# Two graph layers in one kernel: order of the passage between batches, PSUM pairs by turns, and another bank for batch 0's second heads

## The chip, the cores and the metric

The kernel runs on one core of one Trainium2 chip, as one program. The metric is the device time of one execution in microseconds. Before the change it is 3888.36 us (median of 3 runs, 3888.07 to 3892.78).

## What is computed

The input x has 8 batches of 2048 nodes with 256 features; adj is one 2048 x 2048 matrix of zeros and ones, used for all batches. All arithmetic is in f32. Cut to what matters:

```python
# layer 0: 4 heads of 64, softmax within each chunk of 256 keys, summed over 8 chunks
q, k, v = x @ Wq.T + bq, x @ Wk.T + bk, x @ Wv.T + bv
s = clip(q . k / 8, -10, 10);  s = where(adj == 0, -10, s)
ctx = sum over chunks of softmax(s in the chunk) @ v
y = layernorm(ctx @ Wo.T + bo + x) * gamma + beta
x1 = layernorm(x + y)
# layer 1: 4 heads of 64, additive attention over all neighbours
Wh = x1 @ W;  e = leaky_relu(s_src[i] + s_dst[j], 0.2);  e = where(adj, e, -inf)
out = layernorm(x1 + elu(softmax_j(e) @ Wh))
```

## The kernel before

Layer 0 of batch b and layer 1 of batch b-1 run side by side. The loop over b (L854) has 64 **slots** (L870): 4 groups of 512 query nodes, 2 pairs of heads, 8 chunks of 256 keys; 16 slots make one query group. Every engine executes its instructions in the order in which this Python code emits them (a manual schedule, L88); the tile pools and semaphores decide only how long each waits. So the order of the code is the order of the work on each engine.

One slot s does this. `scores(s + 1)` (L350): for each of two 128-key tiles u, two matmuls (one for each head) into a PSUM pair `ps` (2 banks), then on DVE the clip and mask into `pr` (L371). `product(s, 0)` and `product(s, 1)` (L385): the matmuls of one head into `pc`, one bank of pool psC, which has one buffer, and the copy to `raw` on ACT (L400). Between them on ACT stand `exps(s + 1, u)` (L381), two exponentials. `normalize(s - 1)` (L402) stands ahead of the scores: a reciprocal `rd` on DVE, then a product and a sum on POOL.

Between the two products there is the side work of the slot. In batch 0 that is a piece of the mask preparation (`Masks.step`, L201, as long as there are pieces): transposes into `pm` in pool psL, a clip on DVE and a cast `edge` on ACT. From batch 1 on it is `Layer1.step` (L754): three tiles, each with one DVE instruction that makes the edge weights `e` (L689) from `srow`, a row read back from device memory (`rowD`), and 10 or 12 matmuls into `pa` (pool psL, L709). The tiles used in a slot are made in the slot before; three are made ahead of slot 0 (L864). When a unit of layer 1 is finished, `close` (L726) is done in four steps, one for each call of `rest`.

`Between` (L482) takes a finished query group from context to layer 1 input: bias, output projection `po`, add, two norms (statistics on DVE, the power on POOL, the application on ACT), and `values`, the product x1 @ W in `pw`. For groups 0 to 2 its steps are spread over the slots of the next group (tables L570 to L589). `Closing` and `Close` (L760 to L794) do the last norm of layer 1 of two batches before, in the first slots from batch 2 on.

For the last group, and for the projections of the next batch, there is a **passage** between two batches (L923 to L969): the list `order`, written out by hand, 7 times in all. A projection of node group g (`project`, L289) has five pieces: l loads x by 8 DMAs on SP, t turns it on DVE into `xT` (L274), k, v and q are the three products (16 or 8 matmuls each; `linear` L300, `values` L316), each into one PSUM pair of pool psA, which ACT empties. I write k0, v0, q0 for group 0, and so on. `turn_all` (L541) transposes y on PE into a pair (`pt`, L283) and copies it to `x1T`. `factors` gives three small steps for the weights of layer 1.

[...] psA two pairs (one tag, two buffers: the pool chooses which), psC one bank, psL two, psM one. `ps`, `pp`, `pv`, `po` and `pw` of two or four tiles, and `pt` of y share psA.

## Time and profile before

| what | us |
|---|---|
| median of 3 runs | 3888.36 |
| the profiled execution: its time | 3890.5 |
| the profiled execution: its span | 3888.7 |
| batch 0, first scores to last slot | 73 to 414 |
| passages, start of the last `pw` of the slots | 413.8, 871.4, 1334.0, 1794.9, 2256.2, 2717.1, 3178.0 |
| PE busy | 3696.5 (95%) |
| DVE busy | 3204.7 (82%) |
| ACT busy | 1946.2 (50%) |
| POOL busy | 1384.4 (36%) |
| mean granted TensorE clock | 0.992 |

A row of the timeline gives start, length, engine, line, operation, output and inputs, and in brackets the idle time of that engine just before and what ended it. PEld is the loading of weights, which runs beside the matmuls. A matmul in f32 shows as two instructions. Ends of matmuls are modelled, so distances from start to start are the safer measure.

### The profile page before, as it was taken

The page shows a single profiled execution, that of the slowest core. Times are in us where ns is not written, and L with a number is a line of the kernel's source. Part 1 is how long each engine was busy: PE and PEld are TensorE (multiplying, and loading weights), DVE is VectorE, ACT ScalarE, POOL GpSimd, SP SyncE. Part 2 cuts the span into 40 slices and gives each one's busy share as a digit, 9 for nine tenths or more (in the row PEclk, how much of TensorE's full clock was granted, in tenths as well). Part 3 has the DMA queues.
Part 4 walks back from the last instruction along what each step waited for, and adds up shares of the span by engine and source line. Part 5 has one row for each costly group of instructions (what it writes and reads, how often), then busy time and mean ns, then how long its engine had stood idle before and what let it go on. Part 6 is the DMA issues. An engine that isn't in the chain of part 4 may idle for free. (4 is left out here: it accounts for less than half of the span.)

```text
span 3888.7 us, 160154 instructions
## 1 busy us (share of the span) xinstructions
PE 3696.5 (95%) x72068; PEld 2752.5 (71%) x72068; DVE 3204.7 (82%) x4810; ACT 1946.2 (50%) x3601; POOL 1384.4 (36%) x1202
## 2 busy tenths in 40 slices
PE   7988999999999999999999999999999999999787
PEld 4655577776777767776777767777677776776676
DVE  4776499985999779996999959998599977998798
ACT  3655445554555445554555545555455555555321
POOL 0444234342433333432433324434243333434310
PEclk9999999999999999999999999999999999999999
DMA  7642333333434343333433334333343334333354
GB/s 151 150 108 59 77 96 98 97 89 94 121 97 102 75 121 101 99 102 70 134 99 100 97 87 129 101 95 88 94 121 102 98 78 118 106 95 88 95 146 123
DMA packets 771328, 398.48 MB, mean 102 GB/s; under 512 B 442576, under 2 KB 735824, under 8 KB 770640
## 3 DMA queue, kind: packets, MB, share of 16 engines
q1 hardware_dynamic: 720640, 354.54, 35.9%
q10 hardware_dynamic: 50000, 33.70, 2.7%
q8 instruction: 563, 9.22, 1.0%
q14 instruction: 125, 1.02, 0.1%
HBM read 331.22 MB, written 56.89 MB: 100 GB/s over the span
## 5 line engine op out<-in xcount | busy, mean ns | idle before, releaser
L371 DVE SCALAR_TENSOR_TENSOR pr<-ps,slab 128x1024 f32<-128x1024 f32 x1024 | 1192.7, 1205 | 237.3 <-PE ps L360 234.0
L393 PEld LDWEIGHTS pc<-vaug,pr 128*64 128x64 f32 x32768 | 1041.6, 138 | 475.3 <-ACT raw L400 243.9
L689 DVE SCALAR_TENSOR_TENSOR e<-srow,gd,et 128x640 f32<-128x640 f32 (+1 forms) x1536 | 1348.0, 934 | 5.4 <-PE pa L709 5.4
L393 PE MATMUL pc<-vaug,pr 128*64 128x65 f32 x32768 | 1161.4, 224 | 68.9 <-ACT raw L400 63.1
L383 ACT ACTIVATE pr<-pr 128x1024 f32<-128x1024 f32 x1024 | 1052.1, 1057 | 249.3 <-DVE pr L371 234.5
L709 PE MATMUL pa<-waug,e 128*64 128x65 f32 x32768 | 1089.8, 224 | 41.0 <-DVE e L689 39.2
L709 PEld LDWEIGHTS pa<-waug,e 128*64 128x64 f32 x32768 | 1025.2, 139 | 70.3 <-DVE e L689 39.8
L360 PE MATMUL ps<-qT,kT 64*128 64x512 f32 x4096 | 1022.4, 617 | 9.1 <-DVE pr L371 7.0
L415 POOL TENSOR_TENSOR part<-raw,rd 128x512 f32<-128x512 f32 x448 | 467.9, 1044 | 1472.7 <-DVE rd L408 1460.1
L400 ACT COPY raw<-pc 128x260 f32<-128x260 f32 x1024 | 383.5, 375 | 1139.0 <-PE pc L393 1092.4
L417 POOL TENSOR_TENSOR acc<-acc,part 128x512 f32<-128x512 f32 x448 | 574.0, 1281 | 35.2
L360 PEld LDWEIGHTS ps<-qT,kT 64*128 64x128 f32 x4096 | 351.5, 186 | 332.1 <-issue 208.7
L408 DVE RECIPROCAL rd<-raw 128x8 f32<-128x8 f32 x512 | 101.5, 198 | 139.4 <-ACT raw L400 133.2
L415 POOL TENSOR_TENSOR acc<-raw,rd 128x512 f32<-128x512 f32 x64 | 66.8, 1043 | 366.1 <-DVE rd L408 365.3
L304 PE MATMUL pp<-xT,wk_sb 128*128 128x512 f32 x256 | 123.9, 628 | 47.0 <-DVE xT L274 32.3
L737 ACT ACTIVATE hh<-pa,dn 128x64 f32<-128x64 f32 x512 | 114.0, 319 | 101.3 <-DVE dn L733 101.3
L552 PE MATMUL pw<-w_sb,x1T 128*128 128x264 f32 x512 | 137.0, 403 | 2.6 <-DVE x1T L274 2.5
L468 POOL TENSOR_TENSOR rs_c<-rs_c,nhalf 128x4 f32<-128x4 f32 x32 | 55.6, 1738 | 227.5 <-DVE off_c L467 227.5
L508 PE MATMUL po<-wo_sb,qT 128*128 128x256 f32 x512 | 124.8, 389 | 0.0
L304 PEld LDWEIGHTS pp<-xT,wk_sb 128*128 128x128 f32 x256 | 48.3, 198 | 106.5 <-issue 49.6
L320 PE MATMUL pv<-wv_sb,xT 128*128 128x256 f32 x512 | 115.9, 379 | 0.0
L304 PE MATMUL pp<-xT,wq_sb 128*128 128x512 f32 x256 | 115.3, 593 | 0.0
(90 smaller groups left out, 1888.2 us busy)
## 6 DMA issues: line engine op xcount, KB each, us to landing
et<-edgeD SPq DMA_DIRECT2D x256, 320.0 KB, 3.2
slab<-clipD SPq DMA_DIRECT2D x512, 128.0 KB, 3.5
et<-edgeD SPq DMA_DIRECT2D x128, 384.0 KB, 3.5
srow<-rowD SPq DMA_DIRECT2D x64, 320.0 KB, 4.4
xp<-in_x_dram SPq DMA_DIRECT2D x256, 64.0 KB, 2.3
xg<-in_x_dram SPq DMA_DIRECT2D x32, 512.0 KB, 4.7
x1D<-y ACTq DMA_DIRECT2D x32, 512.0 KB, 3.1
x1g<-x1D SPq DMA_DIRECT2D x32, 512.0 KB, 5.9
```

Source lines behind the costliest of these rows:

```text
L304: nc.tensor.matmul(pp[:, c, :], lhsT=w[:, kc, c * P : (c + 1) * P], rhs=st["xT"][:, kc, :], start=(kc == 0), stop=(kc == KC - 1),)
L360: nc.tensor.matmul(ps[:, k, :], lhsT=kT[rows, hp, t * P : (t + 1) * P], rhs=qT[rows, hp, cols], start=True, stop=True,)
L371: nc.vector.scalar_tensor_tensor(pr, pss[u], -CLIP, slab[:, u, :].unsqueeze(1).to_broadcast([P, 2, CH]), op0=ALU.max, op1=ALU.min,)
L383: nc.scalar.activation(pr, pr, AF.Exp, scale=0.125)
L393: nc.tensor.matmul(pc[z * D : (z + 1) * D, i, :], lhsT=probs[s][u][:, k, i * P + z * D : i * P + (z + 1) * D], rhs=vaug[:, KT * c + u, 2 * ...
L400: nc.scalar.copy(raws[s][:, k], pc)
L415: nc.gpsimd.tensor_mul(part, raw[:, :, :, :D], rd.to_broadcast([P, 2, QT, D]))
L417: nc.gpsimd.tensor_add(accv, accv, part)
L508: nc.tensor.matmul(po[:, k, :], lhsT=qT[:, c, t * P : (t + 1) * P], rhs=wo_sb[:, c, :], start=(c == 0), stop=(c == KC - 1),)
L552: nc.tensor.matmul(pw[:, k, : F + 2 * H], lhsT=self.x1T[:, c, u * P : (u + 1) * P], rhs=w1_sb[:, c, :], start=(c == 0), stop=(c == KC - 1),)
L689: nc.vector.scalar_tensor_tensor(e[:, :w], self.rows[n][:, :w], self.gd[:, h, j : j + 1], self.edge[k // JG][:, j % JG, :w], op0=ALU.max, ...
L709: nc.tensor.matmul(self.pa[z * D : (z + 1) * D, i * D1 : (i + 1) * D1], lhsT=e[:, i * P + z * D : i * P + (z + 1) * D], rhs=self.waug[:, j ...
```

## The change

- psA gets two tags with one buffer each, and `two_banks` hands them out strictly by turns.
- For batches after the first, the queries of the last node group (q3) go, half by half, into the two banks of psL.
- In batch 0 `product(s, 1)` uses a bank of psL instead of psC.
- The load of group 0 of the next batch is called in slot 61 instead of 63, and its turn (t0) in slot 63 instead of in the passage.
- The first scores of a batch stand in the passage ahead of q3, their exponentials behind q3 (batch 0 keeps them where they were).
- In the passage, k1 stands ahead of q0, k2 ahead of `turn_all`; the four `lower.rest` steps are spread over the beginning of the passage.

The diff, cut to its core (`...` marks what is left out; the other uses of `two_banks` are the same edit in `transposed`, `values`, `scores`, `output` and `Between.values`):

```diff
-    psA = ctx.enter_context(tc.tile_pool(name="psA", bufs=2, space=bass.MemoryType.PSUM))
+    psA = ctx.enter_context(tc.tile_pool(name="psA", bufs=1, space=bass.MemoryType.PSUM))
...
+    turn_of = [0]
+
+    def two_banks(shape, name):
+
+        turn_of[0] ^= 1
+        return psA.tile(shape, F32, tag=f"psA{turn_of[0]}", name=name)
...
-        def linear(dst, w, bias):
-            pp = psA.tile([P, KC, CH], F32, tag="psA", name="pp")
+        def linear(dst, w, bias, apart=False):
+            if apart:
+                pps = [psL.tile([P, CH], F32, tag="psL", name="pp") for _ in range(KC)]
+            else:
+                pp = two_banks([P, KC, CH], "pp")
+                pps = [pp[:, c, :] for c in range(KC)]
...
-            lambda: linear(qT, wq_sb, bq_sb),
+            lambda: linear(qT, wq_sb, bq_sb, b > 0 and g == NCH - 1),
...
-    def product(s, k):
+    def product(s, k, alone):
...
-        pc = psC.tile([P, QT, D1], F32, tag="psC", name="pc")
+
+        pool, tag = (psL, "psL") if alone and k else (psC, "psC")
+        pc = pool.tile([P, QT, D1], F32, tag=tag, name="pc")
...
-        scores(0)
-        for u in range(KT):
-            exps(0, u)
+            scores(0)
+            for u in range(KT):
+                exps(0, u)
...
-            if s == SLOTS - 1 and b + 1 < B:
+            if s == SLOTS - 3 and b + 1 < B:
                 turns = [project(b + 1, g) for g in range(NCH)]
                 turns[0].pop(0)()
...
+            if s == SLOTS - 1 and b + 1 < B:
+                turns[0].pop(0)()
...
-            product(s, 0)
+            product(s, 0, not lower)
...
-            product(s, 1)
+            product(s, 1, not lower)
...
-        if lower and b + 1 < B:
-            lower.rest(4)
...
-            (t0, k0, v0, q0), (l1, t1, k1, v1, q1), (l2, t2, k2, v2, q2), (l3, t3, k3, v3, q3) = turns
-            order = [begin, t0, lambda: before.values((2, 3)), steps[0], k0, ctx, l1, v0, steps[1]]
-            order += [t1, steps[2], q0, *steps[3:5], k1, l2, steps[5], v1, steps[6], t2, q1, l3]
-            order += [steps[7], k2, steps[8], steps[9], v2, fs[0], t3, q2, fs[1], k3]
-            order += [lambda: [load_slab(s) for s in range(3)], fs[2], v3, q3]
+            (k0, v0, q0), (l1, t1, k1, v1, q1), (l2, t2, k2, v2, q2), (l3, t3, k3, v3, q3) = turns
+            rest = [lambda: lower.rest(1)] if lower else []
+            order = [begin, *rest, l1, *rest, lambda: before.values((2, 3)), *rest, k0, *rest, ctx]
+            order += [v0, steps[0], t1, steps[1], k1, steps[2], q0, *steps[3:5], l2, v1, steps[5]]
+            order += [steps[6], t2, q1, l3, k2, *steps[7:10], v2, fs[0], t3, q2, fs[1]]
+            order += [lambda: [load_slab(s) for s in range(3)], k3, fs[2], v3]
+            order += [lambda: scores(0), q3, lambda: [exps(0, u) for u in range(KT)]]
```

In `order`, steps[0] is the bias, [1] the output projection `po`, [2] its addition, [3] shift and first statistics, [4] the first norm's application, [5] scale, second addition and statistics, [6] the second application and the store, [7] `turn_all`, [8] and [9] the two halves of `values`, and fs the three steps of `factors`.

## Prediction

> **What bounds the kernel now.** I read the page's first part, then the timeline by stretches: the slots of batch 0, the passages between batches, the first slots of a batch. The first line says that TensorE is the engine to follow; DVE, at 82%, has the least room behind it.

> ```profile
> PE 3696.5 (95%) x72068; PEld 2752.5 (71%) x72068; DVE 3204.7 (82%) x4810; ACT 1946.2 (50%) x3601; POOL 1384.4 (36%) x1202
> ```

> In batches 1 to 7 a slot of wide tiles takes 6.03 us with PE closed up (ps 1.92, pc 0.98, pa 2.10, pc 1.03, start to start). PE can be late at three places. The first is the slot of batch 0, which has no layer 1 work (timeline: start, length, engine, line, idle before and its releaser):

> ```profile
> 265.25 0.20 DVE L408 RECIPROCAL rd<-raw 128x8 f32<-128x8 f32 x1 [2.28 <-ACT raw L400]
> 265.37 2.34 DVE L371 SCALAR_TENSOR_TENSOR pr<-ps,slab 128x1024 f32<-128x1024 f32 x2
> ...
> 266.04 1.15 PE L393 MATMUL pc<-vaug,pr 128*64 128x65 f32 x32
> ...
> 267.29 0.38 ACT L400 COPY raw<-pc 128x260 f32<-128x260 f32 x1 [2.14 <-PE pc L393]
> 267.56 2.01 ACT L383 ACTIVATE pr<-pr 128x1024 f32<-128x1024 f32 x2
> ...
> 267.72 1.15 PE L393 MATMUL pc<-vaug,pr 128*64 128x65 f32 x32 [0.53 <-ACT raw L400]
> 268.80 1.99 PE L508 MATMUL po<-wo_sb,qT 128*128 128x256 f32 x8
> ```

> The second head's product waits until ACT has emptied the one bank of psC: 1.68 us from pc to pc, where pc to the next matmul is 1.08. The slot is 1.92 + 1.68 + 1.08 = 4.68.

> The second place is the passage. Its PE rows (from 2 to 3; five of the six with layer 1 read alike):

> ```profile
> 1334.03 2.94 PE L552 MATMUL pw<-w_sb,x1T 128*128 128x264 f32 x12
> 1339.29 3.70 PE L304 MATMUL pp<-xT,wk_sb 128*128 128x512 f32 x8 [2.32 <-DVE xT L274]
> ...
> 1350.17 3.60 PE L304 MATMUL pp<-xT,wq_sb 128*128 128x512 f32 x8
> 1355.12 3.70 PE L304 MATMUL pp<-xT,wk_sb 128*128 128x512 f32 x8 [1.36 <-ACT qT L312]
> ...
> 1367.82 3.70 PE L304 MATMUL pp<-xT,wk_sb 128*128 128x512 f32 x8 [0.94 <-ACT qT L312]
> 1371.35 3.72 PE L552 MATMUL pw<-w_sb,x1T 128*128 128x264 f32 x16
> ```

> Three waits: the first keys (k0) on the turn of the nodes, k1 and k2 on an evacuation of queries, so on a PSUM pair. k1 has been given the pair of q0, which stands just before it.

> The third is the start of a batch from 2 on. DVE begins it late, the closing norms are added, and in slot 1 the edge tiles come late for the next slot's pa, 2.78 us instead of 2.27:

> ```profile
> 949.00 2.87 DVE L689 SCALAR_TENSOR_TENSOR e<-srow,gd,et 128x768 f32<-128x768 f32 x3
> ...
> 950.07 2.78 PE L709 MATMUL pa<-waug,e 128*64 128x65 f32 x72
> ```

> **The change part by part.**

> *Second heads of batch 0 in psL.* This removes the wait for the psC copy. PE then needs 1.92 + 1.08 + 1.08 = 4.08. Does another loop hold the slot? ACT does raw, two exps, raw in order; the second raw frees DVE's rd, which stands ahead of the next pr. By the rows: rd to pr 0.12, two pr 2.34, 0.06 to the last exp, 0.90 to the copy behind it, copy 0.36, 0.10 to rd: 3.88. That is under 4.08, so PE sets the slot and 0.60 is saved. The 30 slots without a mask piece give 18.0. In the other 34 (the last mask transposes start at 256.39) the transposes lie between the products, again 1.68 apart. Five transposes need 0.28 (72.00 to 72.28), so PE would need 4.36 to 4.42; but the loop now holds the mask's evacuation ahead of raw (0.57 for 640 columns, start to start; 0.11 more for 768): 4.48, 4.48, 4.59, mean 4.52. The slot gains 0.16, in sum 5.4. I take 2 off for slots in which ACT applies a norm (2.08) or DVE carries two norm steps. Sum 21.4. Bounds: 9 to 20 for the plain slots (period 4.38 to 4.0), 0 to 9 for mask slots. The masks lose their second bank: their transposes now wait for the evacuation of the slot before (98.18 for transposes at 99.83), so nothing.

> *The turn of the first nodes in slot 63.* The eight loads move from slot 63 to 61, but SP's order stays as it was (nothing else is issued between), and they go out at 859.65 already, landing some 2.3 after the last (864.65). DVE has no pr in slot 63, so the 1.25 is hidden by pc and pa; without that cover it would delay rd. k0 follows pw after 2.77, as in the first passage (413.78 to 416.55), instead of 5.26: minus 2.49.

> *Pairs by turns, new order.* Call E the end of po (1350.17). On PE now: k1, q0, v1, q1, k2, then the transposes of y (pt) and pw; before: q0, k1, v1, q1, pt, k2, pw. All five now wait on evacuations long done, so q1 ends at E+13.77 without the 1.36. But k2 also waits for DVE's third xT, which stands behind the whole norm of y, and the norm's first apply stands on ACT behind q0's evacuation:

> ```profile
> 895.14 2.08 ACT L473 ACTIVATE y<-y,off_a,rs_a 128x256 f32<-128x256 f32 x4 [1.00 <-POOL off_a L469]
> ...
> 901.89 1.25 DVE L274 STREAM_TRANSPOSE xT<-xp 128x1024 f32<-128x1024 f32 x1 [0.16 <-DMA xp<-in_x_dram]
> ```

> There po ended at 889.25, so the apply began at E+5.9 and xT was done 8.0 later. Now q0 ends at E+6.88, its evacuation (0.20 and 1.26) at E+8.34, so xT at E+16.35: k2 waits 2.6. k2 takes 3.54, pt starts at E+20.0 (q1's evacuation, behind the second apply, ends there too) and takes 1.33. Then pw needs x1T: kT's evacuation is through at 21.4, pt's matmuls at 21.3, copy 21.5 to 22.5. pw starts at E+22.6, a wait of 1.2 that k2 used to cover, and takes 3.56 to the values: E+26.1. Before it was 1374.91 - 1350.17 = 24.74. Minus 2.49 plus 1.39: 1.10 saved, in six passages 6.6. In the first there was no wait for k0, and 26.23 from E: 0.1. Sum 6.7; bounds minus 3 (0.5 worse in each) and plus 18 more (if xT is not late).

> *lower.rest spread over the passage.* The same instructions among other ACT and DVE work, with no pr or pa near: nothing. If its h came later, the norm that reads it is a batch away.

> *First scores ahead of q3.* From the end of v3 (T; 928.50 in passage 1): ps u0 0.99, u1 waits for the values' copy (T+1.27) to T+2.26, q3 in psL to T+5.8, second scores to T+7.8. ACT's exps stand behind q3's second evacuation: T+6.0, 0.63, two exps to T+8.7, so the first pc completes at about T+9.5. Before: pc at 936.96, complete at 937.95 = T+9.45. Nothing on PE. But DVE has pr of slot 0 done at T+3.7 and the first edge tiles once srow lands (issued 928.35, median 4.4: T+4.3), so pr of slot 1 starts near T+7.3 instead of T+10.05. The lateness at the third place was 0.5 over what the slack bears; 2.7 less removes both stalls. Slots of 6.60 and 6.72 for 6.03 in batches 2 to 7: 1.25 each, 7.5. Bounds 0 (srow late) and 7.5.

> **The clock.** Windows of 8 us over two k0 with the same 2.3 wait (us, busy of PE, PEld, DVE, ACT, POOL, granted clock, DMA):

> ```profile
> 876.00:884.00 8.00, 7.33 (x20) 4.08 (x21) 2.82 (x3) 1.74 (x3) 0.00 (x0) 0.79 0.42 67
> 1339.00:1347.00 8.00, 7.71 (x30) 5.31 (x31) 2.58 (x3) 1.82 (x4) 0.00 (x0) 1.00 0.42 66
> ```

> One of six ran its first matmuls at half speed, 1.70 lost (5.40 for 3.70); the first passage lost 1.5 at k2. [...] by the rows a wait of 2.3 already trips it one time in six, one of 2.6 perhaps one in four: 7 x 0.25 x 1.7 = 3.0. I take the rows: 3.2 lost before, 3.0 after, nothing.

> **Sum.** 21.4 + 6.7 + 7.5 = 35.6 from the profiled execution's span of 3888.7 (its time is 3890.5, the median of the runs 3888.36; I subtract from the median): 3852.8.

> **Rivals.**
> - *Batch 0 stays held by ACT and DVE.* For it: the loop of 3.88 is only 0.2 under PE's 4.08, and apply or norm steps add to it. Against: the wait named in the row is the psC copy alone. It would leave 5: 3869.
> - *Only batch 0 gains*: the clock trips at most k2 waits (7 x 1.7 = 12), or the starts keep their stalls (7.5) because srow lands late and a second new wait eats the rest. 3867. For it: srow took 3.4 to 8.0 to land; against: e is needed only at T+9.5.
> - *The passage gains more*: k2's wait is not there, since something in the norm chain runs earlier than the old rows say. 18 more: 3835. Against: ACT and DVE work in the order read above.
> - *Slower.* At k2 the clock halves and does not come back: it decides from 35.6 / 7 = 5.1 us lost in each passage, some 10 us at half speed, k2 to pw; the trace has 1.7.
> - *The pairs change nothing*: in the first passage k1 had no wait already, so this can be so there; in the other six the row of 1.36 speaks against it.

> **How the numbers follow.** Main case 0.57, its own range 3844 to 3862. Batch 0 held 0.15, only batch 0 gains 0.14, more in the passage 0.08, slower 0.03, no change 0.03. The range 3838 to 3871 takes in the second and third case, and leaves out most of the fourth and the last two. A measurement of this kernel tells 0.2% (7.8 us) from no change. Faster 0.94, within 0.03, slower 0.03.

> **What would show it.** Plain slots of batch 0 at 4.1 (loop theory: 4.4 or more), mask slots near 4.5; no idle before k0 and k1; k2 after 2.6 on DVE xT, pw after 1.2 on ACT x1T; slots 2 and 5 of batches 2 to 7 at 6.03; first pc no earlier after v3. I am wrong if plain slots stay above 4.4, if k2 has no wait, or if the passage's clock falls below 0.9 in most passages.

## The result, and the profile after

The changed kernel takes 3866.09 us (median of 4 runs, 3862.74 to 3866.61); the kernel before, run beside it, 3890.57 us (3888.07 to 3893.08). The ratio is 0.9935, with a 95% interval of 0.9918 to 0.9952: faster by about 25 us, where I had forecast 35.6. It is inside the range, 13 us slower than the single number. The two profiled spans are 3888.7 and 3861.0, a difference of 27.7.

The first part of the page shows nearly the same busy time as before on every engine. Of the 27.7 us, 19.0 are idle time of PE; its busy time, whose ends are modelled, fell by the other 8.7. The groups below it (busy, mean ns of one, then idle time before them and what ended most of it, in us) show two waits that are new or have another cause: k2 on the turn of the third nodes (seven times 2.44 of the 36.9; most of the rest lies ahead of batch 0), and the layer 1 products `pw`.

```profile
PE 3687.8 (96%) x72068; PEld 2746.0 (71%) x72068; DVE 3204.6 (83%) x4810; ACT 1953.6 (51%) x3601; POOL 1387.4 (36%) x1202
...
L315 PE MATMUL pp<-xT,wk_sb 128*128 128x512 f32 x256 | 124.1, 630 | 36.9 <-DVE xT L281 36.9
L565 PE MATMUL pw<-w_sb,x1T 128*128 128x264 f32 x512 | 138.7, 406 | 17.0 <-ACT x1T L293 9.0
```

The same two groups before:

```profile
L304 PE MATMUL pp<-xT,wk_sb 128*128 128x512 f32 x256 | 123.9, 628 | 47.0 <-DVE xT L274 32.3
...
L552 PE MATMUL pw<-w_sb,x1T 128*128 128x264 f32 x512 | 137.0, 403 | 2.6 <-DVE x1T L274 2.5
```

Lines move by 7 to 13: L304 became L315, L360 L371, L393 L406, L508 L521, L552 L565, L689 L702, L709 L722.

**Where the time went.** I compare the start of the first scores, of the last scores of each batch and of the last `pw` of its slots in the two timelines:

| stretch | before | after | gain | predicted |
|---|---|---|---|---|
| start of the program to batch 0's first scores | 73.29 | 74.54 | -1.25 | 0 |
| batch 0, first scores to the last `pw` | 340.49 | 328.04 | 12.45 | 21.4 |
| six passages, half-speed k0 and k2 set apart | | | 8.3 | 6.6 |
| first passage | | | 0.3 | 0.1 |
| batch starts, batches 1 to 7 | | | 11.2 | 7.5 |
| half-speed k0 and k2 in the six | 1.7 | 5.1 | -3.4 | 0 |
| sum | | | 27.6 | 35.6 |

The first row is not the change's: the kernel before and the run with the first turn alone, below, have the same instructions up to there and start their scores at 73.29 and 75.46; over all the profiles of this study that start lies between 72.9 and 76.0. A passage is taken here from the last `pw` of the slots to its third values: 40.88 before and 39.50 after where no k0 or k2 is at half speed, so 1.38 in each of the six. A period runs from one such `pw` to that of the next batch. The batch starts are the remainder of the six periods (3.2, 3.1, 1.4, 3.0, 3.2, 1.6) and of batch 1 (0.6).

**Batch 0.** A plain slot in the timeline of after, PE alone:

```profile
304.52 1.99 PE L371 MATMUL ps<-qT,kT 64*128 64x512 f32 x8
306.44 2.09 PE L406 MATMUL pc<-vaug,pr 128*64 128x65 f32 x64
308.46 1.99 PE L371 MATMUL ps<-qT,kT 64*128 64x512 f32 x8
```

The two products are one row of 64 matmuls now, and the slot takes 3.94 instead of 4.68. That is better than the 4.08 of the prediction. But in slot 46, the first `pw` of a group (all engines, rows left out):

```profile
308.67 0.37 ACTq L546 DMA_DIRECT2D x1D<-y  x1
...
311.59 4.04 SPq L269 DMA_DIRECT2D x1t<-x1D  x8
...
315.35 2.09 PE L406 MATMUL pc<-vaug,pr 128*64 128x65 f32 x64
...
315.81 2.34 DVE L382 SCALAR_TENSOR_TENSOR pr<-ps,slab 128x1024 f32<-128x1024 f32 x2
...
319.34 1.25 DVE L281 STREAM_TRANSPOSE x1T<-x1t 128x1024 f32<-128x1024 f32 x1 [1.19 <-issue]
320.51 0.16 DVE L421 RECIPROCAL rd<-raw 128x8 f32<-128x8 f32 x1
...
320.64 1.16 PE L565 MATMUL pw<-w_sb,x1T 128*128 128x264 f32 x4 [3.21 <-DVE x1T L281]
```

PE is through with the products at 317.4 and waits until 320.6 for the turn of x1, which stands on DVE behind `pr` and, by its 1.19 of idle, behind the load. The three waits of this kind in batch 0 are 1.98, 3.21 and 2.77; before they were 0.64, 0 and 1.83. The other waits are in the slots with mask pieces and norm steps:

```profile
213.03 0.30 DVE L474 BATCH_NORM_AGGREGATE mv_b<-st_b 128x2 f32<-128x6 f32 x2
...
213.24 0.94 DVE L238 TENSOR_SCALAR clip<-pm 128x768 int8<-128x768 bf16 x1
...
214.22 0.80 ACT L240 CAST edge<-pm 128x768 uint8<-128x768 bf16 x1 [1.94 <-DVE clip L238]
...
215.07 0.44 PE L236 MATMUL pm<-identb,ab 128*128 128x128 bf16 x5 [1.61 <-ACT edge L240]
```

With one bank left to the masks, the next transposes wait for the cast of the ones before, the cast waits for the clip, and the clip stands behind the norm steps on DVE. There are four such waits: 0.38, 1.26, 0.21 and 1.61. The table gives batch 0 in stretches. "Distance n" is here and below the time from the scores of slot n to those of slot n + 1; most of it is the work of slot n - 1, so the late slots 2 and 5 of the prediction are distances 3 and 6, and what the expectations quoted below call slots 2 to 18, 19 to 34 and 14 are distances too.

| distances of batch 0 | before | after | gain |
|---|---|---|---|
| 0, 1 | 14.23 | 14.11 | 0.1 |
| 2 to 18: mask piece, no step of a group | 79.61 | 76.48 | 3.1 |
| 19 to 34: mask piece and steps of a group | 92.31 | 93.95 | -1.6 |
| 35 to 62: no mask piece | 143.90 | 131.99 | 11.9 |
| last scores to the last `pw` | 10.44 | 11.51 | -1.1 |

The loss in distances 19 to 34 is not that of the masks: 31 to 34, where the first wait for x1 stands, take 26.23 instead of 24.06 and lose 2.2; 19 to 30, where the four waits of the masks lie, gain 0.5.

**The passage**, from 2 to 3, on PE:

```profile
1318.76 2.94 PE L565 MATMUL pw<-w_sb,x1T 128*128 128x264 f32 x12
1321.53 3.60 PE L315 MATMUL pp<-xT,wk_sb 128*128 128x512 f32 x8
...
1332.31 3.60 PE L315 MATMUL pp<-xT,wk_sb 128*128 128x512 f32 x8
1335.74 3.60 PE L315 MATMUL pp<-xT,wq_sb 128*128 128x512 f32 x8
...
1342.63 3.60 PE L315 MATMUL pp<-xT,wq_sb 128*128 128x512 f32 x8
1348.67 3.67 PE L315 MATMUL pp<-xT,wk_sb 128*128 128x512 f32 x8 [2.44 <-DVE xT L281]
1352.29 1.09 PE L290 MATMUL pt<-identf,y 128*128 128x128 f32 x8
1354.60 3.83 PE L565 MATMUL pw<-w_sb,x1T 128*128 128x264 f32 x16 [1.22 <-ACT x1T L293]
```

k0 follows `pw` after 2.77 and k1 waits for nothing. k2 waits 2.44 and the second `pw` 1.22, all as predicted. From the end of po (E, 1332.31) to the third values (1358.26) it is 25.95, where the prediction says 26.1. In three of the seven passages k2 also takes 5.37 instead of 3.67.

**The batch start**, batch 3 (its first product, and the edge tiles on DVE):

```profile
1378.19 2.87 DVE L702 SCALAR_TENSOR_TENSOR e<-srow,gd,et 128x768 f32<-128x768 f32 x3 [1.76 <-DMA et<-edgeD]
...
1380.64 0.34 PE L406 MATMUL pc<-vaug,pr 128*64 128x65 f32 x4
...
1381.46 1.04 PE L406 MATMUL pc<-vaug,pr 128*64 128x65 f32 x28 [0.48 <-ACT pr L394]
...
1382.33 2.27 PE L722 MATMUL pa<-waug,e 128*64 128x65 f32 x72
```

The first product is complete no earlier after v3 than before (`pa` begins 9.47 behind v3's end, before 9.44), but DVE makes its first edge tiles ahead of it. The late ones are gone: distances 3 and 6, 6.60 and 6.72 before, and all others from 2 to 13 take 6.03 or 6.04, but for one of 6.19 in batch 2. Distance 14, where the last closing norm stands (slots 11 to 13), was 7.13 in all six batches and takes 6.31 to 6.88.

### The profile page after: what moved, and what is told of

It reads as the page before. It is cut to its first block, busy times and chain, and to the rows that moved or that the text cites. A ratio compares the mean times of both kernels' runs of the same rounds, so it can differ in the third digit from the quotient of the medians.

```text
span 3861.0 us, 160222 instructions
## 1 busy us (share of the span) xinstructions
PE 3687.8 (96%) x72068; PEld 2746.0 (71%) x72068; DVE 3204.6 (83%) x4810; ACT 1953.6 (51%) x3601; POOL 1387.4 (36%) x1202
## 5 line engine op out<-in xcount | busy, mean ns | idle before, releaser
L702 DVE SCALAR_TENSOR_TENSOR e<-srow,gd,et 128x640 f32<-128x640 f32 (+1 forms) x1536 | 1349.6, 934 | 17.9 <-DMA et<-edgeD 12.5
L406 PEld LDWEIGHTS pc<-vaug,pr 128*64 128x64 f32 x32768 | 1040.6, 138 | 445.5 <-issue 245.3
L406 PE MATMUL pc<-vaug,pr 128*64 128x65 f32 x32768 | 1157.9, 224 | 42.6 <-ACT raw L413 35.1
L722 PE MATMUL pa<-waug,e 128*64 128x65 f32 x32768 | 1081.5, 224 | 42.4 <-DVE e L702 40.0
L722 PEld LDWEIGHTS pa<-waug,e 128*64 128x64 f32 x32768 | 1020.1, 139 | 68.1 <-DVE e L702 39.8
L371 PE MATMUL ps<-qT,kT 64*128 64x512 f32 x4096 | 1027.4, 619 | 6.8 <-DVE pr L382 6.5
L371 PEld LDWEIGHTS ps<-qT,kT 64*128 64x128 f32 x4096 | 351.3, 186 | 330.4 <-issue 209.7
L315 PE MATMUL pp<-xT,wk_sb 128*128 128x512 f32 x256 | 124.1, 630 | 36.9 <-DVE xT L281 36.9
L565 PE MATMUL pw<-w_sb,x1T 128*128 128x264 f32 x512 | 138.7, 406 | 17.0 <-ACT x1T L293 9.0
L521 PE MATMUL po<-wo_sb,qT 128*128 128x256 f32 x512 | 125.5, 389 | 2.1 <-DVE qT L448 1.5
L315 PEld LDWEIGHTS pp<-xT,wk_sb 128*128 128x128 f32 x256 | 49.8, 200 | 94.3 <-issue 73.1
L315 PE MATMUL pp<-xT,wq_sb 128*128 128x512 f32 x256 | 116.0, 596 | 0.0
```

The source lines that it names most:

```text
L315: nc.tensor.matmul(pps[c], lhsT=w[:, kc, c * P : (c + 1) * P], rhs=st["xT"][:, kc, :], start=(kc == 0), stop=(kc == KC - 1),)
L371: nc.tensor.matmul(ps[:, k, :], lhsT=kT[rows, hp, t * P : (t + 1) * P], rhs=qT[rows, hp, cols], start=True, stop=True,)
L406: nc.tensor.matmul(pc[z * D : (z + 1) * D, i, :], lhsT=probs[s][u][:, k, i * P + z * D : i * P + (z + 1) * D], rhs=vaug[:, KT * c + u, 2 * ...
L521: nc.tensor.matmul(po[:, k, :], lhsT=qT[:, c, t * P : (t + 1) * P], rhs=wo_sb[:, c, :], start=(c == 0), stop=(c == KC - 1),)
L565: nc.tensor.matmul(pw[:, k, : F + 2 * H], lhsT=self.x1T[:, c, u * P : (u + 1) * P], rhs=w1_sb[:, c, :], start=(c == 0), stop=(c == KC - 1),)
L702: nc.vector.scalar_tensor_tensor(e[:, :w], self.rows[n][:, :w], self.gd[:, h, j : j + 1], self.edge[k // JG][:, j % JG, :w], op0=ALU.max, ...
```

## The experiments

The kernels of one group were timed beside the kernel before on one chip. Ratios are to that; differences from the changed kernel (ratio 0.9935) are ratios subtracted, times 3890, and uncertain by some 9 us, as both ratios have an interval. Where that is too coarse I use the stretches of the profiles. The stretch of batch 0 repeats to 0.15 us in the four profiles with the order of before (330.05 to 330.20), and to 0.6 in four with the order of the change (316.46 to 317.08), in which the half speed differs.

### Batch 0's second heads alone

Added to the kernel before: the bank of psL for the second heads.

```diff
-        pc = psC.tile([P, QT, D1], F32, tag="psC", name="pc")
+        pool, tag = (psL, "psL") if alone and k else (psC, "psC")
+        pc = pool.tile([P, QT, D1], F32, tag=tag, name="pc")
...
```

> The kernel before with one part of the change: the second heads of batch 0 take psL. In the profile of the changed kernel the stretch from batch 0's first scores to its last is 13.5 us shorter (330.05 to 316.53). My theory: this part alone brings that, minus 12 to minus 14 us. Rival, the term of the prediction: minus 21.4. A gain of under 5 would say that batch 0 is held by ACT and DVE in any case.

3877.89 us, ratio 0.9974 (0.9966 to 0.9982), minus 10, or 12 by the medians. The stretch from first to last scores of batch 0 is 313.99 us, 2.5 under the changed kernel's 316.53: distances 31 to 34 take 24.56 instead of 26.23, with less of the half speed there, and distance 1 takes 1.0 less. So this part alone is worth about what it is worth in the change, and not 21.

### The change without it

```diff
-            product(s, 0, not lower)
+            product(s, 0, False)
...
-            product(s, 1, not lower)
+            product(s, 1, False)
```

> The changed kernel with the second heads of batch 0 back in psC: what is left are the passages and the batch starts. From the marks of the two profiles (start of the last pw of each batch's slots) this should be minus 15 us against before, minus 13 to minus 18 as the number of passages that start k2 at half speed differs. By the prediction's terms (6.7 and 7.5) it is minus 14.2; if pairs and passage order change nothing and only the starts do, minus 8 to minus 11.

3872.74 us, ratio 0.9957 (0.9941 to 0.9974), minus 17. Batch 0 takes 330.08, as before. The two parts add up as far as these times can tell: 10 to 12 and 17 are 27 to 29, within the uncertainty of the whole (25).

### The apply of the norm ahead of q0

In the changed kernel, so that ACT applies norm a before it empties q0:

```diff
-            order += [v0, steps[0], t1, steps[1], k1, steps[2], q0, *steps[3:5], l2, v1, steps[5]]
+            order += [v0, steps[0], t1, steps[1], k1, *steps[2:5], q0, l2, v1, steps[5]]
```

> The changed kernel with the apply of norm a emitted ahead of q0 in the passage, so that it stands ahead of q0's evacuation on ACT. My theory: k2's wait of 2.44 us for the third xT comes from there. Then the apply starts at E+5.9 instead of E+8.2, xT is 2.36 earlier, k2 waits at most 0.1, and seven passages are 16.5 us shorter; with the three half-speed k2 gone as well up to 21.6: minus 16.5 to minus 22 against the changed kernel (some 3846). Rival: the chain is held by DVE or POOL or by the loads of the third nodes; then k2 keeps over 1.5 us of wait and the gain is under 6.

3843.71 us, ratio 0.9884 (0.9869 to 0.9899), minus 20 against the changed kernel. Six passages take 62.32 each, scores to scores, instead of 64.64 (66.33 where k2 ran at half speed), and no k2 is slow. The same place in its timeline (E is 1326.04):

```profile
1331.94 2.08 ACT L486 ACTIVATE y<-y,off_a,rs_a 128x256 f32<-128x256 f32 x4 [1.00 <-POOL off_a L482]
...
1333.92 1.24 ACT L323 ACTIVATE qT<-pp,bq_sb 128x512 f32<-128x512 f32 x2
...
1338.69 1.25 DVE L281 STREAM_TRANSPOSE xT<-xp 128x1024 f32<-128x1024 f32 x1 [0.17 <-DMA xp<-in_x_dram]
...
1339.86 2.07 ACT L486 ACTIVATE y<-y,off_b,rs_b 128x256 f32<-128x256 f32 x4 [2.29 <-POOL off_b L482]
...
1340.08 3.67 PE L315 MATMUL pp<-xT,wk_sb 128*128 128x512 f32 x8
```

against these of the changed kernel (E is 1332.31):

```profile
1339.38 1.27 ACT L323 ACTIVATE qT<-pp,bq_sb 128x512 f32<-128x512 f32 x2 [2.17 <-PE pp L315]
...
1340.53 2.07 ACT L486 ACTIVATE y<-y,off_a,rs_a 128x256 f32<-128x256 f32 x4
...
1347.28 1.25 DVE L281 STREAM_TRANSPOSE xT<-xp 128x1024 f32<-128x1024 f32 x1 [0.16 <-DMA xp<-in_x_dram]
```

The apply starts at E+5.90 instead of E+8.22, the turn at E+12.65 instead of E+14.97, and k2 has nothing to wait for. So k2's wait is due to the place of one ACT instruction, as the prediction had read it.

### The turn of x1 and its products one slot later

In the changed kernel, for batch 0 alone: the turn in slot 15 of a group, the single `pw` in slots 15, 0, 1 and 2.

```diff
+    LATER = {0: 1, 1: 2, 2: 3}
...
-                for step in BESIDE.get(i, ()):
+                for step in BESIDE.get(i, ()) if lower or i != 14 else ():
                     step(group)
+                if i == 15 and not lower:
+                    group.turn()
...
-            if before and i in AFTER:
+            if before and i in AFTER and lower:
                 AFTER[i](before)
+            elif before and i in LATER:
+                before.values((LATER[i],))
...
-            if group and i in BEHIND:
+            if group and i in BEHIND and (lower or i < 14):
                 BEHIND[i](group)
+            elif group and i == 15:
+                group.values((0,))
...
-            order = [begin, *rest, l1, *rest, lambda: before.values((2, 3)), *rest, k0, *rest, ctx]
+            first = [] if lower else [lambda: before.values((1,))]
+            order = [begin, *rest, l1, *rest, *first, lambda: before.values((2, 3)), *rest, k0, *rest, ctx]
```

> The changed kernel with batch 0's turn of x1 and the four single pw one slot later (slots 15, 0, 1, 2 instead of 14, 15, 0, 1; for the last group the second one goes to the passage). My theory: the store and reload of x1 take a fixed 10.7 us from the end of the apply to the turn, slots of 3.93 instead of 4.68 no longer cover it, and the three pw waits of 1.98, 3.21 and 2.77 us vanish, with the half-speed matmuls behind two of them: minus 8 to minus 10.6 against the changed kernel (some 3857). Rival: the waits are set by something else on DVE, so they move along with the turn: within 2 us of the changed kernel.

3888.88 us, ratio 0.9997 (0.9989 to 1.0006). The total says little: as the first `elif` is written, it also holds in the later batches, where slot 2 of groups 2 and 3 computes one `pw` a second time, 14 in all, some 15 us. Batch 0 is not touched by that and can be read: 316.37 us against 316.53. My theory fell here. The waits have moved along with the turn:

```profile
323.64 1.24 DVE L281 STREAM_TRANSPOSE x1T<-x1t 128x1024 f32<-128x1024 f32 x1
...
324.93 1.40 PE L565 MATMUL pw<-w_sb,x1T 128*128 128x264 f32 x4 [1.90 <-DVE x1T L281]
```

This turn is not late for its load (no idle time stands before it), and `pw` still waits 1.90. It is the place: the turn stands on DVE behind the scores' tiles of the next slot, and `pw` directly behind the products of this one. In a slot of 3.93 DVE gets there 1.9 later than PE. In the last group the passage begins with a wait of 5.06, since x1 is turned only in the last slot.

### The products one slot behind the turn

So the turn stays in slot 14, and only `pw` moves to slots 15, 0, 1 and 2 in batch 0 (the edit above without its second part, and with `lower` asked in both branches).

> The changed kernel with batch 0's single pw one slot behind the turn of x1 (turn in slot 14 as it was, pw in slots 15, 0, 1, 2; for the last group the second one at the start of the passage); the other batches as they are. My theory after the run with both moved: the wait of pw is one of place, since in a slot of 3.93 us DVE finishes the scores' tiles and the turn behind them 1.9 us after PE is through with the products, and the load of x1 adds up to 1.3. With a slot between them the waits of 7.96 us in batch 0 go, less up to 1 each where DVE now waits for the load: the stretch from first to last scores of batch 0 falls from 316.5 to 309 to 312, and the whole by 5 to 8 us. Rival: the load is late by more than the trace shows, DVE stands still in front of it and PE with it: no gain.

3854.34 us, ratio 0.9903 (0.9888 to 0.9918), minus 12 against the changed kernel. The stretch of batch 0 is 309.27, minus 7.3 (and 20.8 under the 330.05 of before): distances 47 to 50 take 19.06 instead of 23.43, distances 31 to 34 23.32 instead of 26.23. In the timeline:

```profile
316.76 1.25 DVE L281 STREAM_TRANSPOSE x1T<-x1t 128x1024 f32<-128x1024 f32 x1 [1.12 <-issue]
...
316.77 2.09 PE L406 MATMUL pc<-vaug,pr 128*64 128x65 f32 x64
...
318.01 2.31 DVE L382 SCALAR_TENSOR_TENSOR pr<-ps,slab 128x1024 f32<-128x1024 f32 x2
...
318.79 1.16 PE L565 MATMUL pw<-w_sb,x1T 128*128 128x264 f32 x4
```

DVE still stands 1.12 in front of the load, but PE goes from product to `pw` without a pause. The theory after the first attempt holds. The profiled spans differ by 9.7. What lies outside the stretch is the third wait for x1, at the start of the first passage, which is 1.6 shorter apart from its slow k2, and k2 itself, slow in two passages instead of three.

### Mask slots as before

In the changed kernel, the bank of psL only in slots that have no mask piece:

```diff
+            masked = not masks.left()
...
-            product(s, 1, not lower)
+            product(s, 1, not lower and masked)
```

> The changed kernel with the second heads of batch 0 in psL only in slots without a mask piece; mask slots as before, so that the masks have both banks of psL. In the profiles the slots without norm steps (numbers 2 to 18) gained 3.1 us from the second bank, and slots 19 to 34, with norm steps and mask pieces, lost 1.6, since the mask transposes wait for the evacuation of the one before (3.5 us in four slots). My theory: the two nearly cancel, the stretch of batch 0 stays at 316.5 within 2.5 us. Rival, the term of the prediction: mask slots were worth 5.4 us, so it becomes 322.

3868.10 us, ratio 0.9939 (0.9924 to 0.9954), the same as the changed kernel. Distances 0 to 34 take 186.29 us instead of 184.54: 1.75 is what the second bank is worth there as the kernel stands, not 5.4. But distances 31 to 34, with the first wait for x1, take 24.07 here and 26.23 in the change; in 0 to 30 the second bank is worth 3.9. The rest of the stretch's 319.98 against 316.53 is distances 47 to 50, which run 1.7 longer at the waits for x1, the price of one stretch at half speed. I had allowed 2.5 for the stretch and it came out 3.5 longer, so neither number stands alone. The gain in the mask slots is real, and more than half of it is lost again at the wait for x1.

### The first scores back behind q3

In the changed kernel:

```diff
-            order += [lambda: scores(0), q3, lambda: [exps(0, u) for u in range(KT)]]
+            order += [q3, lambda: scores(0), lambda: [exps(0, u) for u in range(KT)]]
```

> The changed kernel with the next batch's first scores back behind q3, everything else as changed. My theory: the head start of DVE is what removed the late slots of batches 2 to 7: in the two profiles slots 2 and 5 gained 1.26, and slot 14, where the closing norm makes the next stall, 0.25 to 0.9. They come back: 6 x 1.8 = plus 11 us against the changed kernel (plus 8 to plus 14, as the number of half-speed k2 differs). Rival, the prediction's term: only slots 2 and 5 are touched, plus 7.5. If pairs by turns and not the head start removed them: within 2 us.

3878.85 us, ratio 0.9967 (0.9954 to 0.9979), plus 12. The late slots are back, one of them as before to the hundredth:

```profile
1397.63 2.78 PE L722 MATMUL pa<-waug,e 128*64 128x65 f32 x72
```

A passage without slow k2 and its batch take 459.25 instead of 457.74: 1.5 in each of six, 9 together. The others run k2 at half speed, six of seven instead of three of seven, which is 5 more. This kernel also keeps a gain that is not the head start's: with q3 in psL its first `pa` begins 9.16 behind v3's end, where it is 9.44 before and 9.47 in the change. So undoing the head start costs 1.5 in each of six, 9 together, and the 0.3 that stays makes up the 1.8 that a batch start gained. The 9 is more than the 7.5 of the prediction, because distance 14 returns to 7.14 as well.

### The exponentials ahead of q3 too

In the changed kernel:

```diff
-            order += [lambda: scores(0), q3, lambda: [exps(0, u) for u in range(KT)]]
+            order += [lambda: scores(0), lambda: [exps(0, u) for u in range(KT)], q3]
```

> The changed kernel with the exps of the first scores emitted ahead of q3, so that they stand ahead of q3's evacuations on ACT. My theory: the first product of each batch, which stops after 4 matmuls and resumes 0.48 us after its weights were due (6.73 us for the slot instead of 6.03), waits for these exps alone: 0.7 x 7 = minus 4.9 us. Rival: DVE, which waits for the edge tiles at this point, holds the next slot, so that the 0.7 comes back there: within 1.5 us of the changed kernel.

3864.19 us, ratio 0.9929 (0.9914 to 0.9943), within the uncertainty of the changed kernel. The first product no longer stops, and distance 1 falls from 6.73 to 6.03:

```profile
1379.34 2.88 DVE L702 SCALAR_TENSOR_TENSOR e<-srow,gd,et 128x768 f32<-128x768 f32 x3 [1.72 <-ACT qT L323]
...
1381.82 1.15 PE L406 MATMUL pc<-vaug,pr 128*64 128x65 f32 x32
```

But in batch 4 distance 6 now takes 6.38, distance 10 6.07 and distance 14 7.14 instead of 6.88: 0.65 of the 0.70 comes back. DVE's first edge tiles begin 5.3 behind v3's end in both kernels; PE came earlier, DVE did not, and while it carries the closing norms it has no room to catch up. Only batch 1, which has none, keeps its 0.7. The rival was right, though I had expected the loss in the next slot.

### Pairs by turns alone

On the kernel before, psA as two tags by turns, nothing else.

> The kernel before with PSUM pairs by turns and nothing else. My theory after reading the passages again: k1's wait of 1.36 us goes in six passages, but the transposes of y then come 1.36 earlier and wait for the norm, as they do in the first passage of the kernel before, which has no wait at k1 and 1.03 + 0.94 ahead of k2: end of po to the third values is 24.7 us there too. So nothing: within 3 us of before. Rival, as the prediction counted it: 6 x 1.36 = minus 8.

3893.05 us, ratio 1.0005 (0.9997 to 1.0014): nothing. k1 has lost its wait in every passage, and the transposes of y take it up:

```profile
1349.60 3.60 PE L311 MATMUL pp<-xT,wk_sb 128*128 128x512 f32 x8
...
1360.64 0.33 PE L290 MATMUL pt<-identf,y 128*128 128x128 f32 x1 [0.55 <-ACT y L480]
...
1363.82 3.70 PE L311 MATMUL pp<-xT,wk_sb 128*128 128x512 f32 x8 [0.94 <-ACT qT L319]
```

From the end of po (1346.17) to the third values (1370.92) it is 24.75, before 24.74.

### The first turn alone

On the kernel before, the load of the first nodes in slot 61 and their turn in slot 63.

```diff
-            if s == SLOTS - 1 and b + 1 < B:
+            if s == SLOTS - 3 and b + 1 < B:
                 turns = [project(b + 1, g) for g in range(NCH)]
...
+            if s == SLOTS - 1 and b + 1 < B:
+                turns[0].pop(0)()
...
-            order = [begin, t0, lambda: before.values((2, 3)), steps[0], k0, ctx, l1, v0, steps[1]]
+            order = [begin, lambda: before.values((2, 3)), steps[0], k0, ctx, l1, v0, steps[1]]
```

> The kernel before with one part of the change: the first nodes are loaded in slot 61 and turned in slot 63 instead of after it; order and pairs as before. My theory: k0 follows pw after 2.77 us instead of 5.26 in six passages, the norm chain that starts at the end of po moves with it, so all of it stays: 6 x 2.49 = minus 15, and up to 1.7 more if the half-speed k0 goes. Then the new order, k1 ahead of q0, has given back some 1.4 us in each passage of the change. Rival: something else in the passage (loads, the closing norms) gives it back: minus 7 or less.

3874.54 us, ratio 0.9955 (0.9940 to 0.9969), minus 16.5 by the medians. Passages 2 to 7 take 66.87, scores to scores, instead of 69.45, one like the other; k1 still waits 1.36 and k2 0.94.

All of the 2.5 stays (2.58 in each). In the change the new order has given 1.2 of it back in each passage, and the new wait at k2 is often followed by half speed, which this kernel never shows in the six.

### Three edits together

The apply ahead of q0, `pw` one slot behind the turn in batch 0, the exponentials ahead of q3.

> The changed kernel with three edits together: the apply of norm a ahead of q0, batch 0's single pw one slot behind the turn, the exps of the first scores ahead of q3. They touch different places. If they add up: minus 22.4, minus 11.8 and minus 1.9 against the changed kernel, some 3831 us (3828 to 3836). If they share a cause (half-speed matmuls counted twice): 3838 to 3842.

3834.19 us, ratio 0.9852 (0.9835 to 0.9868): 57 us faster than before and some 32 faster than the change. The stretch of batch 0 takes 310.73, the seven passages 62.08 to 62.33, and no k2 runs at half speed. They add up: the expectation for that was 3828 to 3836.

## Why the prediction was right, and where it was off

- **Sign and mechanism were right**, but for the pairs by turns, which bring nothing alone. The other places moved as described, and each of the two parts is faster alone. That the sum of the table is only 8 us off owes something to errors of opposite sign: batch 0 fell short by 9.0 and half speed took 3.4, the batch starts brought 3.7 and the passages 1.7 more.
- **Batch 0 is the mis-sized term: 21.4 predicted, 12.4 measured.** The loop question was answered rightly: a slot with nothing beside it went to 3.94. (It is 0.14 under my 4.08 because two products in a row cost 2.0; I had charged 1.08 twice, the distance from a product to a matmul of another kind.) What failed is the sentence "I take 2 off for slots in which ACT applies a norm (2.08) or DVE carries two norm steps": it puts the wait of `pw` for x1 at nothing. The turn of x1 on DVE and `pw` on PE stand so close, and the store and reload ahead of the turn take so long (10.2 to 12.0 us from the end of the apply to the turn before, 10.3 to 10.7 after), that only the longer slot covered most of it. PE waits 7.96 instead of 2.47, and half speed follows two of the three waits. With `pw` moved by one slot the stretch from first to last scores gains 20.8 against before, so this wait is nearly the whole miss. Two smaller costs are missing as well. "So nothing" for the masks' second bank rested on one row of a slot without norm steps; in slots with them the transposes wait 3.46 in all, and distances 2 to 30 gain 3.7 where 29 x 0.16 is 4.6. And of the 28 distances without mask piece eight with norm steps stay at 4.20 to 4.32 and four with a `po` gain 0.1 or 0.4; with distance 47, which holds a `pw` and loses 2.5, all 28 gain 11.9 where 28 x 0.60 less 2 is 14.8.
- **The passage was right**: 1.38 saved in each of six, predicted 1.10; k2's wait 2.44 for 2.6, `pw`'s 1.22 for 1.2. The runs split it more sharply: the turn of the first nodes brings 2.6 each, pairs by turns nothing, the new order takes 1.2 back. The rival "the pairs change nothing" was right about the pairs, and for a reason I had in the rows of the first passage: without the wait at k1 the transposes of y wait for the norm.
- **The first scores** brought more than 7.5. I counted the stalls in slots 2 and 5 and not the one at the last closing norm. The batch starts show 11.2, of which 0.6 are batch 1's, and undoing the head start takes back 9.
- **The clock**: I said nothing in sum (3.2 lost before, 3.0 after). But 1.5 of the 3.2, the slow k2 of the first passage, is also in its 26.23, so it was counted twice; by my own numbers the balance was minus 1.3. After it is 5.1 in k2 alone, and in the six passages 3.4 more than before.
- Of the rivals, "batch 0 held by ACT and DVE" was right in part: PE sets the plain slots, DVE and its neighbours those with other work. The rival by which only batch 0 gains is refuted by the run without it (minus 17). k2's wait is there, so the passage did not gain more; the run with the apply moved shows what it would have been worth, 20 us. The slower case did not come: half speed at k2 costs 1.70 and ends there.

## What to carry to other kernels

When a slot gets shorter, every distance counted in slots gets shorter too: list what is placed "one slot later" (a reload, a turn on another engine, a buffer to be emptied) and compare each with the new length, above all in the slots that carry more than the repeated work. A wait that is removed from the middle of a passage is only won if the chain that ends it moves as well: here the turn ahead of the norm chain won all of its 2.5 us in each passage, the wait behind it (1.36) nothing. And where a new wait falls on an engine, look for the one instruction in the releasing chain that stands behind work nobody needs yet; moving the apply ahead of one evacuation was worth nearly as much as the whole change.

## What was not expected of the hardware

Waits of 2.43 to 2.45 us ahead of k2 were followed by half speed in 24 of 49 passages (seven profiles with that wait: 3, 3, 4, 6, 3, 2 and 3 of seven); waits of 2.32 ahead of k0 in 3 of 18 (the kernel before, batch 0's heads alone, pairs alone). I had taken one in four. Here is a slow k2 of the changed kernel; a usual one, at 1348.67, is shown above. The windows below stand over the wait and behind it, first for the slow one, then for the usual one (us, busy of PE, PEld, DVE, ACT, POOL, granted clock, DMA share, GB/s):

```profile
889.24 5.37 PE L315 MATMUL pp<-xT,wk_sb 128*128 128x512 f32 x8 [2.44 <-DVE xT L281]
```

```profile
885.98:889.39 3.41, 0.97 (x3) 0.19 (x2) 2.91 (x11) 0.38 (x1) 1.21 (x2) 1.00 0.60 94
889.39:892.81 3.42, 3.42 (x5) 1.36 (x5) 0.00 (x0) 2.96 (x6) 0.00 (x0) 0.50 0.81 187
1346.78:1350.19 3.41, 1.52 (x4) 0.83 (x5) 1.54 (x4) 1.74 (x4) 1.21 (x2) 1.00 0.78 123
1350.19:1353.60 3.41, 3.19 (x14) 1.46 (x12) 0.00 (x0) 2.82 (x6) 0.00 (x0) 1.00 0.75 237
```

Behind the waits of 1.61 and 1.98 in batch 0 the granted clock was 0.70 over 5 us and 0.59 over 4 us. The 3.21 at 320.64, longer than any of these, was followed by scores of the usual 1.99. So in these runs the length of one wait does not decide.

On average the half speed behind a wait of 2.4 us ahead of k2 costs 0.8 us in these runs (24 in 49, 1.5 to 1.7 each).
